# Two tiles of every third group copied on chip instead of every fourth, with ACT joining a column of both tables in one ACTIVATE

## The chip, the cores and the metric

The kernel runs on one core of a Trainium2 chip. The metric is the time on the device in microseconds (us), of which lower is better. The engines are named as the profile names them: PE (TensorE) multiplies matrices, DVE (VectorE), ACT (ScalarE) and POOL (GpSimd) work on elements, and SP issues DMAs. Each has its own queue of instructions and works through it in order.

## The reference

One layer of a graph network with a residual and a layer norm: 12,500 nodes of 64 features, 200,000 edges sorted by destination, 32 features per edge.

```python
msg_in = concatenate([nodes[row], nodes[col], edge_features])   # row = src, col = dst
messages = relu(msg_in @ mW1 + mb1) @ mW2 + mb2
aggregated = segment_sum(messages, col)
out = relu(concatenate([nodes, aggregated]) @ uW1 + ub1) @ uW2 + ub2
x = layernorm(x + out)
```

## The kernel before

The first product is split over its three inputs. Two tables are made at the start: tab_a is x times the source part of mW1, tab_b is x times the destination part. Edges are worked in tiles of 128 and in groups of six tiles; there are 261 groups (index s below), and two groups share what is loaded and selected at once.

*Sources.* For most tiles POOL fetches the rows of tab_a by the edges' source numbers, one indirect DMA per tile (gather, line 207), into the tile xg of the group. The first ten groups fetch rows of x instead. Nine buffers of xg are used in turn, so POOL can run ahead of the work; a buffer is free again after the group's h add.

*Copied tiles.* In the groups of the list COPIED the last two of the six tiles aren't gathered. x lies transposed in SBUF, too: xtop holds it in partitions 0 to 63 with zeros below, xbot in partitions 64 to 127 with zeros above. For a copied group a tile xc of 128 by 128 is put together column by column: the upper half of column e is x of the source of edge e of the fifth tile, the lower half that of edge e of the sixth. PE then multiplies it with w1a (line 366) into the sums of pc. Source numbers are read into registers from two lists that DVE works out once from the column list, `cols` (columns_list, in iteration 9). ACT makes the first 64 columns of xc: for each 32-bit word of its list two COPYs of 64 partitions by one float (lines 328 and 330), for two columns of one half, so 128 COPYs. DVE makes the other 64 columns, each with one bitwise OR of a column of xtop and one of xbot (line 341). The register loads are TENSOR_LOADs (lines 321 and 334; DVE's takes the list in pieces of up to 16 columns, which are 32 words). The work for a copied group is cut into as many shares as there are groups between two copied ones, and `copies(s)` puts one share at the end of each iteration; the last is done two iterations before the group's edge part.

*An iteration s*, with the order written out by hand, puts into the queues: gathers whose buffers are free by then; the norm of an update, if one is due; the destination rows from tab_b (windows); `node_part(s)`, in which DVE adds pc and xg (the h add, line 390, or 386 in a copied group) and ACT applies relu (391, or 387 and 388); `collect(s - 1)`, in which PE sums h into windows of 32 nodes (sums, 418) and counts edges (423); in every second iteration DVE's selections of the next two groups (233, 235, 239) and ACT's cast of one of them (247); `edge_part(s + 1)`, PE's products of destination rows and edge features into pc (363); and the copies.

*Updates.* The sums of up to 448 nodes are kept in PSUM. When a period of nodes ends, ACT takes the sums out (437, 438), PE carries the overlap over (431, 432) and computes the node update (pu, 460 and 461, then py, 469 and 470), DVE takes the statistics (st and mv, 474 and 476), ACT the root (sd, 478), and in the next iteration DVE writes the norm (rs and o, 484 and 487), which frees py's buffer in PSUM for a further pc. As the first nodes have the most edges, periods are long at first (47 groups) and get shorter. New ones begin at groups 47, 66, 81, 93, 104, 114, 123, 131, 139, 146, 153, 160, 166, 172, 178, 184, then every five groups from 190 to 225, and every four to 257.

Of the kernel before, what the change touches and what calls it, by code (L numbers as in the profile page):

```python
# [10 lines left out]
F32 = mybir.dt.float32  # L11
I32 = mybir.dt.int32
AF = mybir.ActivationFunctionType
ALU = mybir.AluOpType
# [3 lines left out]
P = 128  # L18
N, D, DE, DH = 12500, 64, 32, 128
# [10 lines left out]
NSUB = -(-NT // SUB)  # L30
# [39 lines left out]
XBASE = 8320  # L70
U8, U16 = mybir.dt.uint8, mybir.dt.uint16
YBASE = XBASE + 4 * XCOLS
FIRST, GAPS = 20, (4,)
COPIED = []
while FIRST + sum(GAPS) * (len(COPIED) // len(GAPS)) + sum(GAPS[:len(COPIED) % len(GAPS)]) < NSUB - 12:
    COPIED.append(FIRST + sum(GAPS) * (len(COPIED) // len(GAPS)) + sum(GAPS[:len(COPIED) % len(GAPS)]))
RNDS = -(-len(COPIED) // len(GAPS))
SINGLE = 64


def updates():
# [17 lines left out]
def gnn_kernel(ctx: ExitStack, tc: tile.TileContext, x1T, x, eT, e_rows, src, src_row, dst, dst_row, wlist, wrow, wnext, whalf,  # L99
# [24 lines left out]
    nc = tc.nc  # L124
    const = ctx.enter_context(tc.tile_pool(name="const", bufs=1))
# [10 lines left out]
    xbot = const.tile([P, XCOLS], F32, name="xbot")  # L136
# [2 lines left out]
    past = const.tile([1, 1], F32, name="past")  # L139

    cols = const.tile([RNDS * len(GAPS), 2 * P], I32, name="cols")
    col_i = const.tile([RNDS * len(GAPS), SINGLE, 2], U16, name="col_i")
    col_a = const.tile([RNDS * len(GAPS), P - SINGLE, 2], I32, name="col_a")
    w1b = const.tile([P, DH], F32, name="w1b")
    b1 = const.tile([P, DH], F32, name="b1")

# [65 lines left out]
    with tc.tile_pool(name="sup", bufs=2) as sup, tc.tile_pool(name="work", bufs=2) as work, tc.manual_schedule():  # L212
# [73 lines left out]
        def columns_list():  # L286

            for r in range(len(GAPS)):
                v = src_row[:, ((FIRST + sum(GAPS[:r])) * SUB + SUB - 2) * P:]
                nc.sync.dma_start(cols[r * RNDS:(r + 1) * RNDS],  # L290
                                  bass.AP(v.tensor, v.offset, [[sum(GAPS) * SUB * P, RNDS], [1, 2 * P]]))
            cv = cols.rearrange("k (b e) -> k b e", b=2)
            iv = col_i.rearrange("k (b e) h -> k b e h", b=2)
            nc.vector.tensor_scalar(iv[:, :, :, 0], cv[:, :, :SINGLE:2], 4.0, float(XBASE), op0=ALU.mult, op1=ALU.add)
            nc.vector.tensor_copy(iv[:, :, :, 1], cv[:, :, 1:SINGLE:2])
            for b, base in enumerate((XBASE, YBASE)):
                nc.vector.tensor_scalar(col_a[:, :, b], cv[:, b, SINGLE:], 4.0, float(base), op0=ALU.mult, op1=ALU.add)

        x8, y8 = xtop.bitcast(U8), xbot.bitcast(U8)

        def shares(total, n, of):

            at = [-(-total * i // (n * of)) * of for i in range(n + 1)]
            return [(at[i], min(at[i + 1], total)) for i in range(n)]

        def copies(s):

            for j, c in enumerate(COPIED):
                gap = GAPS[(j - 1) % len(GAPS)]
                if c - 2 - gap <= s < c - 2:  # L310
                    break
            else:
                return
            q = s - (c - 2 - gap)
            k = j % len(GAPS) * RNDS + j // len(GAPS)
            if q == 0:
                xc[c] = work.tile([P, P], F32, name="xc")
            o8 = xc[c].bitcast(U8)
            last_a = 4 * (N - 1)
            lo, hi = shares(SINGLE, gap, 4)[q]  # L320
            _, v = nc.values_load_multi_w_load_instructions(  # L321
                col_i.rearrange("k e b -> k (e b)").bitcast(I32)[k:k + 1, lo:hi], engines=[ET.Activation],
                min_val=0, max_val=N * 65536 - 1, skip_runtime_bounds_check_because="sources are node numbers")
            for i, w in zip(range(lo, hi), v):
                b, e = divmod(i, SINGLE // 2)
                o = o8[b * D:b * D + D, 8 * e:8 * e + 8]
                n = (w & 65535).with_bounds(min_val=XBASE, max_val=XBASE + last_a) - XBASE
                nc.scalar.copy(o[:, :4], x8[:D, bass.ds(n, 4)])  # L328
                n = (w >> 16).with_bounds(min_val=0, max_val=N - 1) * 4
                nc.scalar.copy(o[:, 4:], x8[:D, bass.ds(n, 4)])  # L330
            lo, hi = shares(P - SINGLE, gap, 2)[q]
            for a in range(lo, hi, 16):
                m = min(a + 16, hi)
                _, v = nc.values_load_multi_w_load_instructions(
                    col_a.rearrange("k e b -> k (e b)")[k:k + 1, 2 * a:2 * m], engines=[ET.DVE], min_val=XBASE,
                    max_val=YBASE + last_a, skip_runtime_bounds_check_because="sources are node numbers")
                for e in range(a, m):
                    i, n = (w.with_bounds(min_val=base, max_val=base + last_a) - base
                            for w, base in zip(v[2 * (e - a):], (XBASE, YBASE)))
                    w = 4 * (SINGLE + e)  # L340
                    nc.vector.tensor_tensor(o8[:, w:w + 4], x8[:, bass.ds(i, 4)], y8[:, bass.ds(n, 4)],  # L341
                                            op=ALU.bitwise_or)

        xc = {}
# [297 lines left out]
        def rest(s):  # L642
# [5 lines left out]
            if s == 9:  # L648
                columns_list()
# [78 lines left out]
        for s in range(last + 2):  # L728
# [32 lines left out]
            if s + 2 in due:  # L761
                columns(due[s + 2])
            rest(s)
            copies(s)
            if s - 1 in due:
                store(due[s - 1])
# [4 lines left out]
    with tc.If(flag > 0), tc.tile_pool(name="gen", bufs=1) as up:  # L771
# [28 lines left out]
        with tc.For_i(0, NT, 1) as t:  # L800
# [31 lines left out]
            h = up.tile([P, DH], F32, name="hg")  # L832
# [29 lines left out]
        with tc.For_i(0, NB, 1) as c:  # L862
# [24 lines left out]
            o = up.tile([P, D], F32, name="o")  # L887
# [49 lines left out]
```

## Time and profile before

| | |
|---|---|
| runs | 1834.96, 1829.88, 1831.20 us; median 1831.2 |
| profiled execution | 1832.05 us, its span 1830.3 us |
| POOL | busy 1369.6 us (75%), 1447 gathers |
| PE | busy 1440.8 us (79%), mean granted clock 0.577 |
| ACT | busy 1157.8 us (63%), of which copies 1412.8 us summed one by one (they overlap) |
| DVE | busy 856.1 us (47%) |
| DMA | 108 GB/s on average |
| chain that ended last | POOL 36%, issue 23%, PE 19%, DMA 10%, DVE 7%, ACT 3% |

The busy time is the time in which an engine had an instruction under way. Register work, register loads and the issue of DMAs don't count as busy; where an engine stands idle through them, the waits are put down to "issue". In the lines of groups, the numbers behind the bar are the busy time, the mean duration of one instruction in ns, and the idle time just before them with what ended it. The lines of the chain give the start in us, the length in us, and the engine, tile and line.

### The profile page before, as it was taken

The numbers are of one execution on the slowest core, as the hardware profiler recorded it, in microseconds if no ns is written. First come the engines' busy times: TensorE is split into PE (matmuls) and PEld (weight loads), VectorE is DVE, ScalarE is ACT, GpSimd is POOL, SyncE is SP. The second block draws the span as 40 slices with busy tenths as digits, with TensorE's granted clock in tenths as the row PEclk, the third lists the DMA queues.
The fourth block names the chain that finished last, engine by engine and source line by source line (L and its number), as shares of the span: only waits on it lengthen the run. The fifth ranks groups of instructions, "written<-read, shape, count | busy, mean of one in ns | idle before, by whom it ended". The sixth has DMA issues, their size and how long they took to land.

```text
span 1830.3 us, 51040 instructions
## 1 busy us (share of the span) xinstructions
PE 1440.8 (79%) x9446; PEld 1243.3 (68%) x9446; DVE 856.1 (47%) x4895; ACT 1157.8 (63%) x8032; POOL 1369.6 (75%) x1456
## 2 busy tenths in 40 slices
PE   3697897776777777777877788887888888888887
PEld 3586887676666666666766667776766766767765
DVE  1565664454444444435444445444444544544432
ACT  0224886676676767757766667676776776767511
POOL 7777777777777777777777777777777777777774
PEclk8755655555555555555555555555556556566565
DMA  8874444333333333333333333433343433444432
GB/s 212 202 147 123 125 125 120 96 90 91 90 93 94 95 91 94 101 92 98 100 100 102 99 102 100 107 104 100 106 106 101 110 103 101 109 107 108 109 103 63
DMA packets 209512, 197.52 MB, mean 108 GB/s; under 512 B 58284, under 2 KB 174079, under 8 KB 209199
## 3 DMA queue, kind: packets, MB, share of 16 engines
q0 software_dynamic: 46304, 92.96, 20.4%
q1 hardware_dynamic: 148350, 92.34, 18.5%
q10 hardware_dynamic: 14546, 8.93, 1.8%
q8 instruction: 90, 1.47, 0.3%
q14 instruction: 222, 1.82, 0.3%
HBM read 176.40 MB, written 17.66 MB: 106 GB/s over the span
## 4 chain that ended last, share of the span: by engine, by line
POOL 36%; issue 23%; PE 19%; DMA 10%; DVE 7%; ACT 3%; ACTq 1%; DVEq 1%; SPq 1%; POOLq 0%
POOL xg L207 36%; PE sums L418 7%; DMA xg<-tab_a,src_s 5%; PE pc L363 4%; DVE xc L341 2%; PE pu L460 2%; PE pu L461 1%; DMA tab_a<-tb 1%; DMA l<-in_dst_row 1%; DVE h L390 1%; DVE l L235 1%; PE py L469 1%; PE py L470 1%; ACTq L321 1%; ACT xc L328 1%
## 5 line engine op out<-in xcount | busy, mean ns | idle before, releaser
L207 POOL DMA_INDIRECT xg<-tab_a,src_s x1387 | 1310.8, 945 | 422.7 <-issue 402.0
L418 PE MATMUL sums<-sel,h 128*128 128x32 f32 x3126 | 665.9, 381 | 191.7 <-ACT h L391 186.7
L418 PEld LDWEIGHTS sums<-sel,h 128*128 128x128 f32 x3126 | 635.5, 307 | 254.5 <-ACT h L391 228.8
L328 ACT COPY xc<-xtop 64x4 uint8 x3712 | 698.4, 188 | 114.1 <-issue 112.8
L330 ACT COPY xc<-xtop 64x4 uint8 x3712 | 714.4, 192 | 10.9 <-issue 10.9
L363 PE MATMUL pc<-rhs,l 64*128 64x128 f32 x3126 | 421.5, 424 | 134.8 <-DVE o L487 113.4
L363 PEld LDWEIGHTS pc<-rhs,l 64*128 64x128 f32 x3126 | 349.9, 305 | 191.7 <-DVE o L487 117.1
L341 DVE TENSOR_TENSOR xc<-xtop,xbot 128x4 uint8 x3712 | 299.6, 155 | 278.4 <-issue 278.1
L390 DVE TENSOR_TENSOR h<-pc,xg 128x768 f32<-128x768 f32 (+1 forms) x194 | 183.6, 947 | 355.5 <-DMA xg<-tab_a,src_s 263.4
L391 ACT ACTIVATE h<-h 128x768 f32<-128x768 f32 (+1 forms) x194 | 162.2, 837 | 245.9 <-DVE h L390 235.4
L235 DVE TENSOR_TENSOR l<-l,cps 128x768 f32<-128x768 int32 (+1 forms) x134 | 127.8, 954 | 29.4 <-DMA l<-in_dst_row 25.1
L247 ACT CAST selb<-sel 128x384 bf16<-128x384 f32 x131 | 66.1, 505 | 68.0 <-DVE sel L239 62.0
L474 DVE BATCH_NORM_STATS2 st<-py 128x6 f32<-128x64 f32 x131 | 20.5, 218 | 145.0 <-PE py L470 141.7
L423 PE MATMUL cnt<-selb,one 128*1 128x32 bf16 x1563 | 84.8, 188 | 0.0
L239 DVE TENSOR_TENSOR sel<-cps,drc 128x384 f32<-128x384 f32 x131 | 71.9, 549 | 20.2 <-PE sums L418 19.3
L478 ACT ACTIVATE sd<-mv,eps 128x4 f32<-128x4 f32 (+1 forms) x33 | 9.8, 297 | 109.4 <-DVE mv L476 109.4
L207 POOL DMA_INDIRECT xg<-in_x,src_s x60 | 57.7, 962 | 19.1 <-issue 18.0
L423 PEld LDWEIGHTS <-one 128*1 128x1 bf16 x1563 | 54.0, 83 | 22.5 <-issue 8.7
L386 DVE TENSOR_TENSOR h<-pc,xg 128x512 f32<-128x512 f32 x58 | 39.8, 686 | 49.4 <-DMA xg<-tab_a,src_s 29.5
L460 PE MATMUL pu<-sums_s,w2u 128*128 128x448 f32 (+1 forms) x66 | 61.2, 1032 | 0.5 <-ACT sums_s L437 0.5
L469 PE MATMUL py<-ux,xw 128*128 128x64 f32 x262 | 54.0, 289 | 5.1 <-ACT hTu L462 4.9
L470 PE MATMUL py<-u,hTu 128*128 128x64 f32 x262 | 52.5, 283 | 0.4 <-ACT hTu L462 0.4
(105 smaller groups left out, 857.3 us busy)
## 6 DMA issues: line engine op xcount, KB each, us to landing
l<-in_dst_row SPq DMA_DIRECT2D x262, 96.0 KB
l<-in_eT SPq DMA_DIRECT2D x262, 96.0 KB
xg<-tab_a,src_s POOLq DMA_INDIRECT x1387
rhs<-tab_b SPq DMA_DIRECT2D x361, 32.0 KB
tab_b<-tb SPq DMA_DIRECT2D x13, 512.0 KB
rhs<-tab_b SPq DMA_DIRECT2D x387, 16.0 KB
tab_a<-tb ACTq DMA_DIRECT2D x12, 512.0 KB
out<-o SPq DMA_DIRECT2D x32, 128.0 KB
```

The costliest lines, as they stand in the source:

```text
L207: nc.gpsimd.indirect_dma_start(out=a[:, i, :] if s < XG else a[:, i // 2, i % 2, :], out_offset=None, in_=A[:, :] if s >= XG else x[:, :], ...
L235: nc.vector.tensor_tensor(l[r], l[r].bitcast(I32), node[r].unsqueeze(2).broadcast_to([r.stop - r.start, SUP // 2, P]), op=ALU.is_equal)
L328: nc.scalar.copy(o[:, :4], x8[:D, bass.ds(n, 4)])
L330: nc.scalar.copy(o[:, 4:], x8[:D, bass.ds(n, 4)])
L341: nc.vector.tensor_tensor(o8[:, w:w + 4], x8[:, bass.ds(i, 4)], y8[:, bass.ds(n, 4)], op=ALU.bitwise_or)
L363: nc.tensor.matmul(pc[:, b, k, :], L[g][q:q + 64, m, :], rhs[g % 2][q:q + 64, w, :], start=s >= XG or k == 0, stop=s >= XG and not copied)
L390: nc.vector.tensor_tensor(h[:, b, :m], pc[:, b, :m], a[:, b, :m], op=ALU.add)
L391: nc.scalar.activation(h[:, b, :m], h[:, b, :m], AF.Relu)
L418: nc.tensor.matmul(ps[:, bass.ds(ws[i], WIN)], h[:, i % 2, i // 2, :], S[g][:, k0 + i, :], start=False, stop=ends and i == n - 1)
L423: nc.tensor.matmul(pn[:, bass.ds(ws[i], WIN)], one, SB[g][:, k0 + i, :], start=False, stop=ends and i == n - 1)
L460: nc.tensor.matmul(pu, w2u, sums_s[u % 2][:, :n], start=True, stop=False)
L469: nc.tensor.matmul(py[:, i], xw[u % 2][:, i * P:(i + 1) * P], ux, start=True, stop=False)
```

## The change

Copied groups go from every fourth, from the 20th to the 248th (58 groups), to every third, from the 16th to the 253rd (80 groups). ACT's part of a column list becomes 60 columns and DVE's 68, in three shares instead of four. ACT's columns are made by one ACTIVATE each: its input is the column of xtop and its bias the column of xbot, so that both halves are written at once. The list for ACT changes its form with that: each 32-bit word holds the place in xtop in its lower half and the node number for xbot in the upper half.

```diff
-FIRST, GAPS = 20, (4,)
+FIRST, GAPS = 16, (3,)
...
-while FIRST + ... < NSUB - 12:
+while FIRST + ... < NSUB - 6:
...
-SINGLE = 64
+ACTS = 60
...
-            iv = col_i.rearrange("k (b e) h -> k b e h", b=2)
-            nc.vector.tensor_scalar(iv[:, :, :, 0], cv[:, :, :SINGLE:2], 4.0, float(XBASE), op0=ALU.mult, op1=ALU.add)
-            nc.vector.tensor_copy(iv[:, :, :, 1], cv[:, :, 1:SINGLE:2])
+            nc.vector.tensor_scalar(col_i[:, :, 0], cv[:, 0, :ACTS], 4.0, float(XBASE), op0=ALU.mult, op1=ALU.add)
+            nc.vector.tensor_copy(col_i[:, :, 1], cv[:, 1, :ACTS])
...
-            lo, hi = shares(SINGLE, gap, 4)[q]
+            lo, hi = shares(ACTS, gap, 4)[q]
...
-            for i, w in zip(range(lo, hi), v):
-                b, e = divmod(i, SINGLE // 2)
-                o = o8[b * D:b * D + D, 8 * e:8 * e + 8]
-                n = (w & 65535).with_bounds(min_val=XBASE, max_val=XBASE + last_a) - XBASE
-                nc.scalar.copy(o[:, :4], x8[:D, bass.ds(n, 4)])
-                n = (w >> 16).with_bounds(min_val=0, max_val=N - 1) * 4
-                nc.scalar.copy(o[:, 4:], x8[:D, bass.ds(n, 4)])
-            lo, hi = shares(P - SINGLE, gap, 2)[q]
+            for e, w in zip(range(lo, hi), v):
+                i = (w & 65535).with_bounds(min_val=XBASE, max_val=XBASE + last_a, guaranteed_mod_val=0, out_of_modulus=4) - XBASE
+                n = (w >> 16).with_bounds(min_val=0, max_val=N - 1)
+                nc.scalar.activation(xc[c][:, e:e + 1], x8[:, bass.ds(i, 4)].bitcast(F32), AF.Identity,
+                                     bias=xbot[:, bass.ds(n, 1)])
+            lo, hi = shares(P - ACTS, gap, 2)[q]
             for a in range(lo, hi, 16):
                 m = min(a + 16, hi)
```

In the rest of the function SINGLE becomes ACTS.

More of the change, by code (lines that the diff above doesn't have):

```diff
@@ L72 @@
 YBASE = XBASE + 4 * XCOLS
-FIRST, GAPS = 20, (4,)
+FIRST, GAPS = 16, (3,)
 COPIED = []
-while FIRST + sum(GAPS) * (len(COPIED) // len(GAPS)) + sum(GAPS[:len(COPIED) % len(GAPS)]) < NSUB - 12:
+while FIRST + sum(GAPS) * (len(COPIED) // len(GAPS)) + sum(GAPS[:len(COPIED) % len(GAPS)]) < NSUB - 6:
     COPIED.append(FIRST + sum(GAPS) * (len(COPIED) // len(GAPS)) + sum(GAPS[:len(COPIED) % len(GAPS)]))
 RNDS = -(-len(COPIED) // len(GAPS))
-SINGLE = 64
+ACTS = 60
 def updates():
@@ L141, in gnn_kernel @@
     cols = const.tile([RNDS * len(GAPS), 2 * P], I32, name="cols")
-    col_i = const.tile([RNDS * len(GAPS), SINGLE, 2], U16, name="col_i")
-    col_a = const.tile([RNDS * len(GAPS), P - SINGLE, 2], I32, name="col_a")
+    col_i = const.tile([RNDS * len(GAPS), ACTS, 2], U16, name="col_i")
+    col_a = const.tile([RNDS * len(GAPS), P - ACTS, 2], I32, name="col_a")
     w1b = const.tile([P, DH], F32, name="w1b")
@@ L292, in columns_list @@
             cv = cols.rearrange("k (b e) -> k b e", b=2)
-            iv = col_i.rearrange("k (b e) h -> k b e h", b=2)
-            nc.vector.tensor_scalar(iv[:, :, :, 0], cv[:, :, :SINGLE:2], 4.0, float(XBASE), op0=ALU.mult, op1=ALU.add)
-            nc.vector.tensor_copy(iv[:, :, :, 1], cv[:, :, 1:SINGLE:2])
+            nc.vector.tensor_scalar(col_i[:, :, 0], cv[:, 0, :ACTS], 4.0, float(XBASE), op0=ALU.mult, op1=ALU.add)
+            nc.vector.tensor_copy(col_i[:, :, 1], cv[:, 1, :ACTS])
             for b, base in enumerate((XBASE, YBASE)):
-                nc.vector.tensor_scalar(col_a[:, :, b], cv[:, b, SINGLE:], 4.0, float(base), op0=ALU.mult, op1=ALU.add)
+                nc.vector.tensor_scalar(col_a[:, :, b], cv[:, b, ACTS:], 4.0, float(base), op0=ALU.mult, op1=ALU.add)
         x8, y8 = xtop.bitcast(U8), xbot.bitcast(U8)
@@ L339, in copies @@
                             for w, base in zip(v[2 * (e - a):], (XBASE, YBASE)))
-                    w = 4 * (SINGLE + e)
+                    w = 4 * (ACTS + e)
                     nc.vector.tensor_tensor(o8[:, w:w + 4], x8[:, bass.ds(i, 4)], y8[:, bass.ds(n, 4)],
```

## The prediction

> **What bounds the kernel now.** I read the groups by shape first, then the waits, then single source lines, and last the chain of waits in a late stretch. The groups:
>
> ```profile
> L207 POOL DMA_INDIRECT xg<-tab_a,src_s x1387 | 1310.8, 945 | 422.7 <-issue 402.0 <-DMA xg<-tab_a,src_s 10.4 <-DVE xc L341 3.0
> L330 ACT COPY xc<-xtop 64x4 uint8 x3712 | 714.4, 192 | 10.9 <-issue 10.9
> L341 DVE TENSOR_TENSOR xc<-xtop,xbot 128x4 uint8 x3712 | 299.6, 155 | 278.4 <-issue 278.1
> L478 ACT ACTIVATE sd<-mv,eps 128x4 f32<-128x4 f32 x32 | 9.5, 297 | 106.1 <-DVE mv L476 106.1
> ```
>
> POOL never waits: 945 ns busy and 0.30 us of issue per gather, so one starts every 1.2495 us in the timeline. All 1447 gathers (60 read x) take 1808 of the 1830.3 us. Before such a gather its buffer has been free for some 50 us from group 48 on, nine groups being buffered. So POOL sets the time, as long as the consumers (DVE's h add, ACT's relu, PE's sums) hold its pace of 22 gathers, 27.49 us, per four groups. Do they? The chain from 1560 to 1720 us:
>
> ```profile
> 1612.36 2.02 issue
> 1614.38 1.26 DVE xc L341 x16
> 1616.92 1.81 PE pc L363 x12
> 1619.15 2.70 PE sums L418 x12
> 1622.10 1.58 PE pc L363 x12
> 1623.69 2.70 PE sums L418 x12
> 1626.64 1.58 PE pc L363 x12
> 1628.76 2.77 PE sums L418 x12
> 1632.94 1.79 PE pu L460 x2
> 1634.73 1.20 PE pu L461 x2
> 1635.93 0.87 PE pc L363 x12
> 1638.76 0.62 DVE st L474 x4
> 1639.67 2.02 issue
> 1641.69 1.28 DVE xc L341 x16
> ```
>
> No gather is in it. Here an update comes every four groups, and from one xc to the next pass 27.31, 27.57 and 27.98 us: 27.6, POOL's own pace. The consumers are full too. The loop runs: PE's py, DVE's st, the list load and copies that stand before the norm, norm, h add, relu, copies, relu, copies, relu, sums, update, py. PE and ACT both run through without a gap in its middle. So there are two limits at nearly the same height, and the change lowers one and raises the other.
>
> **The change part by part.** *Gathers.* Copied groups: 58 (20 to 248) become 80 (16 to 253), so 44 gathers go: 44 x 1.2495 = 55.0 us off POOL, none of it covered. POOL alone would give 1832.05 - 55.0 = 1777 us. (The profiled execution took 1832.05, 0.85 over the median of the runs shown.) Its new pace is 16 gathers per three groups, 6.66 us per group against 6.87.
>
> *Lists and copies: the lines.*
>
> ```profile
> L334 DVEq TENSOR_LOAD <-col_a x232: 2097/2152/2719, 159.8 to 1709.2; - x116
> L321 ACTq TENSOR_LOAD <-col_i x232: 1010/1034/1424, 158.2 to 1710.8; - x116
> L328 ACTq ALU_OP  x3712: 35/35/49, 159.5 to 1715.1; - x196
> L330 ACTq FUSED_REGOPS  x3712: 64/67/83, 159.6 to 1715.2; - x196
> ```
>
> *DVE, per group.* Today 16 columns: one load of 32 words (2.15 us), of which the waits show 278.1/232 = 1.2 us, then 16 copies 73 ns apart. After it 68 columns over three steps, cut in pairs: 24, 22, 22; the inner loop takes 16 at a time, so a second load follows. A load of one word takes 0.312 us (line 769), 32 take 2.15, so 59 ns a word and 0.96 to 1.20 us for 12 or 16 words. In today's trace a load starts with four or five copies still queued, which hides 0.3; seen: 0.65 to 0.9. With six or eight more copies (0.44, 0.58) a step grows by 1.05 to 1.45, I take 1.2. Bounds: 0.5, if the load were hidden as the first half of today's is, and 2.6, if it cost a whole 2.15.
>
> *ACT, per group.* Today 16 words give 32 copies in 3.46 us (single rows of the timeline, 105 ns apart, 188 to 192 ns long). Each word costs the sequencer 35 and 67 ns of register work and two dispatches, 209 ns by the trace's starts. After it 20 words give 20 ACTIVATEs of 128x1 with a register for the input and one for the bias. No such instruction is in the trace, so its spacing is bounded. From below: 155 ns, if the two register operations follow each other without a gap and one dispatch (53 ns) remains. From above by the sequencer: 209, if dropping a dispatch saves nothing. By the engine: sd is the nearest row, 297 ns for four elements with a bias against 192 for four without, so a bias adds 105; copies overlap by 92, which leaves 205 if the bias is not overlapped, and about 100 if it is. I take 190 ns, between 155 and the two upper ends but nearer these, as sd is the only row of the same form. That makes 20 x 0.19 + 0.1 = 3.9 us, and four more words in the load 0.2 (50 ns a word, by 286 ns for one and 1034 for 16). An ACT step grows by 0.64 us (bounds: -0.06 at 155 ns, 1.02 at 209).
>
> The Trainium skill (ScalarE: Activation LUTs, What ACT_TABLE_LOAD costs) speaks against the new form: a pointer bias adds about 93 ns to an ACTIVATE, and neighbours overlap by about 93, so one with a bias takes the room of two without. By its figures the spacing would be an estimated 187 ns, the step 0.06 us less than mine and the sum some 3 us lower; sd's 105 ns agrees with the rule.
>
> *PE.* Each copied group adds four matmuls of 64x128, 0.80 us in the timeline, now in every third group: 0.07 us per group. In the late loop PE will wait for ACT, which covers it; uncovered it is 0.27 per four groups. *Start.* Copies begin at iteration 11 instead of 14, while the consumers still trail by 30 to 39 us. The buffer of a gather there is free 18 to 27 us early; three steps and a slower catch-up take some 15 of that. I count nothing, at worst 5 us. The column list (80 rows for 58) goes by the same single DMA on SP, and its conversions stay four DVE operations of about 0.19 us.
>
> *The sum.* The late loop holds one DVE step (py waits for the norm, and edge_part, sums and the next h add are queued behind both) and two ACT steps (relu is queued behind the copies, and PE's sums wait for relu): 27.6 + 1.2 + 2 x 0.64 = 30.1 us per four-group period, where POOL now needs 26.66. A further group in a longer period costs an ACT step: 4.66 to 4.95 us between relus today, 5.4 after, against POOL's 6.66. So the consumers fall back by 3.4 us in a four-group period, 2.2 in one of five (35.5 against 33.3), 0.9 in one of six (40.9 against 40.0), and hold in one of seven. By the list of updates there are five of six groups (160 to 190), seven of five (to 225) and 6.5 of four until copying ends at iteration 250: 4.5 + 15.4 + 22.1 = 42 us. That fits into the 50 us of buffers, so POOL does not stop, but the lag is added at the end. From group 252 on POOL needs 49 x 1.2495 = 61.2 us, and the consumers, without load and copies in their loop (27.6 - 3.3 = 24.3 per four groups, 6.1 each), 54.9: 6.3 are won back. Net 55.0 - 42 + 6.3 = 19.3 us: 1832.05 - 19.3 = 1812.7, **1813 us**.
>
> **The rivals.** *The consumers keep up.* If ACTIVATEs start 155 ns apart, an ACT step does not grow, and PE's own chain binds: 27.6 + 1.2 + 0.27 = 29.1 per four groups and 4.9 for a further one. The lag is 6.5 x 2.4 + 7 x 0.7 = 20, less 6: 1791; with the DVE load hidden as well 1785, and 1777 is the floor. For it: the step drops twelve of 32 instructions. Against it: each column keeps both register operations, and sd's 297 ns.
>
> *The ACT step grows past the gain: slower.* The place is the copies between two relus. The turning point: at 205 ns a step grows by 0.94, the periods fall back by 4.0, 3.1, 2.1 and 1.2 us (four to seven groups), together 62, and the gain is gone: 1832. A further register operation of 35 ns for the bias's address, or for reading bytes as floats, would make it 225 ns: 31.5 per four groups, 6.1 for each further one, so that all periods of up to eleven groups fall back, together 99: 1832 - 55 + 99 - 6 = 1870 us. Were the bias read wholly serial at 297 ns, every group would be ACT's, and it would be over 1950. For it: 205 and 209 are my own upper ends, 15 ns from my value. Against it: today's shift and multiply already share one operation of 67 ns, and the new address needs the same two.
>
> *The change doesn't do what it says* would need POOL to stop gaining, by stalls at the start; that is priced above at 5 us and no case of its own.
>
> **How the numbers follow.** Forecast, 1790 to 1835: 0.50. Consumers keep up, 1777 to 1790: 0.17. ACT past the gain, above 1835: 0.33. The predicted time is the first one's, 1813. Its own range of 1790 to 1835 covers the bounds of the two steps nearest to it. The range given, 1782 to 1880, reaches into both rivals: the lower leaves out 0.07, the upper 0.12 (over 225 ns). A difference of 0.3%, 5.5 us, is about what a measurement of this kernel can tell from none, so faster ends at 1825.7 and slower begins at 1836.7. Of the forecast's 0.50, 0.41 is faster, 0.07 same, 0.02 slower; the second gives 0.17 faster; of the third 0.03 is same, 0.30 slower. Together 0.58, 0.10, 0.32.
>
> **What would show it.** In the profile of the changed kernel: 1343 gathers from tab_a, still 945 ns, but now with idle time that names DVE if the lag passes 50 us; h add's waits for gathers (263.4 us today) falling most after 1100 us; the ACTIVATEs some 190 ns apart, 20 in 3.9 us; two list loads per step, the second near 1.0 us; the chain of waits through ACT's xc from about group 160. A spacing above 205 ns, or POOL waiting for DVE's h adds over much of the second half, makes me wrong on the slow side; gathers that set h add's start to the end, on the fast side.

## The result: 0.3% slower

The changed kernel takes 1836.49 us (median of 7 runs, 1834.92 to 1838.37), the kernel before 1830.36 in the same comparison (1829.39 to 1834.96). The ratio is 1.003, with a 95% interval of 1.0018 to 1.0041: a small loss where a gain of 1% was forecast. The profiled execution took 1838.37 us, its span 1836.6, 6.3 more than the span of before. (The ratios here and below leave out one slow execution, of e4_one_load, that took 1891.81 us where its other three took 1823.74 to 1827.31.)

Groups by shape, after:

```profile
L207 POOL DMA_INDIRECT xg<-tab_a,src_s x1343 | 1273.3, 948 | 421.2 <-issue 386.1 <-DMA xg<-tab_a,src_s 11.9 <-DVE h L387 10.1
L326 ACT ACTIVATE xc<-xtop,xbot 128x1 f32 x4800 | 973.6, 290 | 172.5 <-issue 166.0 <-DMA u<-in_uW 6.5
L338 DVE TENSOR_TENSOR xc<-xtop,xbot 128x4 uint8 x5440 | 450.8, 156 | 407.0 <-issue 406.0
L387 DVE TENSOR_TENSOR h<-pc,xg 128x768 f32<-128x768 f32 x170 | 162.4, 955 | 74.2 <-DMA xg<-tab_a,src_s 24.6 <-PE pc L360 23.3 <-issue 8.7
```

The 44 gathers are gone, and the rest cost nearly what they did, 948 ns on average instead of 945. Two entries have changed: POOL now waits for DVE's h adds (10.1 us, against 1.5 before), and the h adds wait 24.6 us for gathers where the waits of the kernel before have:

```profile
DVE h L390 <- DMA xg<-tab_a,src_s: 263.4, 87, 7.0
```

The gathers no longer lead.

Single source lines (duration in ns: least, median, most; then the start of the first and of the last). First line: the kernel before; the others: after.

```profile
L207 POOL DMA_INDIRECT xg<-tab_a,src_s x1387: 940/944/1973, 78.9 to 1811.1; - x199
```
```profile
L207 POOL DMA_INDIRECT xg<-tab_a,src_s x1343: 942/947/1870, 78.9 to 1772.1; - x192
L320 ACTq TENSOR_LOAD <-col_i x240: 1236/1275/1701, 130.0 to 1763.2; - x120
L326 ACTq ALU_OP  x4800: 35/35/49, 131.8 to 1768.6; - x192
L331 DVEq TENSOR_LOAD <-col_a x480: 843/2052/2533, 124.8 to 1765.7; - x160
```

The last starts of the gathers give the account. POOL's saving of 55.0 us would bring the last gather from 1811.1 to 1756.1; it starts at 1772.1, so it is 16.0 us *late*. From the last gather to the end of the span it was 1830.3 - 1811.1 = 19.2 us and is now 1836.6 - 1772.1 = 64.5, so the *tail* is 45.3 longer. 16.0 + 45.3 - 55.0 = 6.3, the whole difference. These two numbers are given below for every kernel. Not all of the 16.0 us is waiting. In three places, shown below, POOL waits for an h add, 11.1 us beyond its pace; the other 5 us or so are the gathers themselves, which start 1.252 us apart (median) where before's start 1.249 apart. In e1 and e4 below the gathers are as slow, POOL never waits so, and the last gather is 4.5 and 4.7 us late all the same.

When the time was lost is seen from the start of the h adds against the kernel before: 30.0 us earlier at group 160, 23.4 at 190, 9.3 at 226, then 8.7 *later* at group 250. The lag of an h add behind the last gather of its group, taken just before an update, is 14.2 us at group 48 (1.7 before), as the work there still trails from the start, stays at 2 to 3.4 us from group 67 to 161, and is then 5.8, 8.1, 10.8, 13.2 and 15.8 (at 191), 36.5 at 226 and 54.7 at 250. Towards the end of this the buffers are used up, as POOL's timeline shows (start, length, idle time before it and what ended it; a third such wait, of 3.35 us, ends at 1738.97):

```profile
1677.45 0.95 POOL L207 DMA_INDIRECT xg<-tab_a,src_s  x1 [5.05 <-DVE h L387]
1708.34 0.95 POOL L207 DMA_INDIRECT xg<-tab_a,src_s  x1 [3.64 <-DVE h L387]
```

The chain of waits of after, in the same stretch as shown for before:

```profile
1608.84 0.62 DVE st L471 x4
...
1609.74 1.98 issue
1611.72 0.67 DVE xc L338 x8
1612.46 0.56 DVE xc L338 x7
1613.02 0.45 issue
1613.47 0.70 DVE xc L338 x8
...
1615.39 0.88 DVE h L387
1616.35 0.84 ACT h L388
1617.20 0.76 ACTq L320
...
1622.14 0.61 ACT h L384
...
1628.80 2.77 PE sums L415 x12
...
1639.94 0.63 DVE st L471 x4
```

From one st to the next pass 31.1 us, where POOL needs 26.66 for four groups. Between st and the h add stand two list loads (1.98 and 0.45 us of issue) and 24 copies. The relus of three groups follow at 1616.35, 1622.14 and 1627.92, 5.8 us apart, with ACT's list load and its 20 ACTIVATEs between them. In before's chain PE's pc and sums filled this middle; here PE waits for ACT.

### The profile page after: what moved, and what is told of

The parts are those of the page before. It is cut to its first block, busy times and chain, and to the rows that moved or that the text cites. A ratio compares the mean times of both kernels' runs of the same rounds, so it can differ in the third digit from the quotient of the medians.

```text
span 1836.6 us, 52710 instructions
## 1 busy us (share of the span) xinstructions
PE 1437.5 (78%) x9534; PEld 1236.9 (67%) x9534; DVE 1001.0 (55%) x6623; ACT 1305.7 (71%) x5430; POOL 1331.9 (73%) x1412
## 4 chain that ended last, share of the span: by engine, by line
POOL 23%; issue 22%; PE 18%; ACTq 8%; DVE 8%; DMA 6%; ACT 6%; DVEq 2%; SPq 0%; POOLq 0%
POOL xg L207 23%; PE sums L415 6%; DMA xg<-tab_a,src_s 5%; ACTq L326 5%; ACT xc L326 4%; ACTq L320 3%; PE pc L360 3%; DVE xc L338 3%; PE pu L457 2%; PE pu L458 2%; DVEq L331 1%; PE py L466 1%; DVE h L387 1%; PE py L467 1%; DVE l L235 1%
## 5 line engine op out<-in xcount | busy, mean ns | idle before, releaser
L207 POOL DMA_INDIRECT xg<-tab_a,src_s x1343 | 1273.3, 948 | 421.2 <-issue 386.1
L326 ACT ACTIVATE xc<-xtop,xbot 128x1 f32 x4800 | 973.6, 290 | 172.5 <-issue 166.0
L415 PEld LDWEIGHTS sums<-sel,h 128*128 128x128 f32 x3126 | 626.3, 303 | 249.2 <-ACT h L388 157.7
L338 DVE TENSOR_TENSOR xc<-xtop,xbot 128x4 uint8 x5440 | 450.8, 156 | 407.0 <-issue 406.0
L387 DVE TENSOR_TENSOR h<-pc,xg 128x768 f32<-128x768 f32 (+1 forms) x172 | 163.0, 948 | 74.2 <-DMA xg<-tab_a,src_s 24.6
L388 ACT ACTIVATE h<-h 128x768 f32<-128x768 f32 (+1 forms) x172 | 142.0, 827 | 58.3 <-DVE h L387 58.3
L247 ACT CAST selb<-sel 128x384 bf16<-128x384 f32 x131 | 65.8, 502 | 40.2 <-DVE sel L239 37.3
L207 POOL DMA_INDIRECT xg<-in_x,src_s x60 | 57.6, 960 | 19.2 <-issue 17.7
L457 PE MATMUL pu<-sums_s,w2u 128*128 128x448 f32 (+1 forms) x66 | 61.2, 1032 | 0.5 <-ACT sums_s L434 0.5
L383 DVE TENSOR_TENSOR h<-pc,xg 128x512 f32<-128x512 f32 x80 | 55.1, 689 | 10.6 <-DMA xg<-tab_a,src_s 7.8
L363 PE MATMUL pc<-w1a,xc 64*128 64x128 f32 x320 | 60.3, 397 | 0.0
L459 ACT ACTIVATE hTu<-pu,ub_s 128x448 f32<-128x448 f32 (+1 forms) x33 | 20.9, 633 | 49.8 <-PE pu L458 49.8
L458 PE MATMUL pu<-xw,uz 128*128 128x448 f32 (+1 forms) x66 | 54.1, 924 | 0.0
```

The source lines that it names most:

```text
L207: nc.gpsimd.indirect_dma_start(out=a[:, i, :] if s < XG else a[:, i // 2, i % 2, :], out_offset=None, in_=A[:, :] if s >= XG else x[:, :], ...
L326: nc.scalar.activation(xc[c][:, e:e + 1], x8[:, bass.ds(i, 4)].bitcast(F32), AF.Identity, bias=xbot[:, bass.ds(n, 1)])
L387: nc.vector.tensor_tensor(h[:, b, :m], pc[:, b, :m], a[:, b, :m], op=ALU.add)
L388: nc.scalar.activation(h[:, b, :m], h[:, b, :m], AF.Relu)
L415: nc.tensor.matmul(ps[:, bass.ds(ws[i], WIN)], h[:, i % 2, i // 2, :], S[g][:, k0 + i, :], start=False, stop=ends and i == n - 1)
L457: nc.tensor.matmul(pu, w2u, sums_s[u % 2][:, :n], start=True, stop=False)
```

## The experiments

The theory: the consumers' loop, with two ACT steps and one DVE step in each update period, has become slower than POOL from group 160 on; the lag fills the buffers, and at the end it has to be worked off. The rivals: the new ACTIVATEs cost by themselves wherever they are; or the longer list does, by what it does at the start, on PE or in the DMAs.

All ratios are to the kernel before, in runs of the same comparison:

| kernel | gathers saved | ratio, 95% interval | last gather late, us | tail, us |
|---|---|---|---|---|
| before | 0 | 1 | 0 | 19.2 |
| after | 44 | 1.003 [1.0018, 1.0041] | 16.0 | 64.5 |
| e1_form_alone | 0 | 0.9999 [0.9989, 1.0008] | 4.5 | 17.7 |
| e2_list_alone | 44 | 1.0147 [1.013, 1.0164] | 41.9 | 64.0 |
| e3_no_bias | 44 | 0.9803 [0.9787, 0.9819] | 0.5 | 36.5 |
| e4_one_load | 44 | 0.9948 [0.9928, 0.9967] | 4.7 | 64.7 |
| e5e_dve_first | 44 | 0.9822 [0.9806, 0.9839] | -0.7 | 38.9 |
| e7c_late_fourth | 22 | 0.9858 [0.984, 0.9876] | 0.0 | 19.2 |
| e8d_both | 32 | 0.9782 [0.9766, 0.9799] | 0.1 | 18.9 |

The last two columns are from the profiled executions, worked out as above (1811.1 less 1.25 us per gather saved is the start that a last gather would have). The gathers of after, e1, e2 and e4 take 948 ns on average and start 1.252 to 1.253 us apart, those of the others 944 to 946 ns and 1.249 us, so in these four rows some 5 us of the first column are slower gathers and no wait. Why there are two paces is open.

### The two halves of the change, one by one

e1, in after: ACT's new form with the old list (58 groups) and ACT's old share of 64 columns.

```diff
-FIRST, GAPS = 16, (3,)        -ACTS = 60      (... < NSUB - 6)
+FIRST, GAPS = 20, (4,)        +ACTS = 64      (... < NSUB - 12)
```

> The new ACT form with the old list (58 groups, every fourth, 64 columns for ACT, so 16 ACTIVATEs a step). Two limits: POOL sets the time, the consumers (h add, relu, sums, update) follow at its pace. The ACT step is 16 x 0.19 = 3.1 us of copies against 3.46, DVE and the gathers are as before: 1828 to 1831 us, no change. The form itself costs: if ACTIVATEs with a bias register slowed ACT or its neighbours by more than the 0.3 us gained, the late periods would lag and it would be over 1836.

e2, in before: the new list (80 groups) with the old form, ACT making 60 columns by pairs of COPYs.

```diff
-FIRST, GAPS = 20, (4,)        -SINGLE = 64    (... < NSUB - 12)
+FIRST, GAPS = 16, (3,)        +SINGLE = 60    (... < NSUB - 6)
```

> The new list (80 groups, every third, 60 columns for ACT) with the old form, two COPYs per word. The list makes the loss: ACT's step has 40 COPYs at 209 ns a pair, 4.2 us, against 4.0 to 4.3 for 20 ACTIVATEs measured in the changed kernel, so the same late lag, 1836 to 1850 us. The form makes the loss: with COPYs instead the kernel falls clearly below 1830.

Measured: e1 0.9999, e2 1.0147. In e1 a share of 16 columns took 3.32 us on average against 3.57 before, and its h adds still waited 263.7 us for gathers: the gathers set the time, and a shorter share beside them is worth nothing. In e2 a share took 4.43 us, and the consumers held POOL back most, in ten places by 37 us in all (groups by shape, e2):

```profile
L207 POOL DMA_INDIRECT xg<-tab_a,src_s x1343 | 1273.0, 948 | 447.5 <-issue 383.1 <-DVE h L390 22.8 <-DVE cps L233 11.0
```

So, by the ratios, the list alone is a loss of 27 us, more than was expected (1862.83 us against 1836 to 1850), and the new form takes 21 of them back. The form does not cost by itself; it is worth nothing until the list makes ACT's share part of the bound.

### Less in ACT's step, less in DVE's step

e3 leaves out the lower half of ACT's 60 columns, so its ACTIVATEs read no bias, and of the two register operations of each only the ALU_OP of 35 ns is left.

```diff
-                nc.scalar.activation(..., AF.Identity, bias=xbot[:, bass.ds(n, 1)])
+                nc.scalar.activation(..., AF.Identity)
```

> The changed kernel without the bias of ACT's ACTIVATE and its register work; this leaves out the lower half of ACT's 60 columns of each copied pair. ACT's step falls from 4.0-4.3 to about 2.1 us of ACTIVATEs (one register operation and one dispatch, 88 to 100 ns each). If ACT's step between two relus is what binds the late periods, they shrink from 30.7 us per four groups to the 29 of PE and DVE, and the time falls to 1785-1800 us. If DVE's step binds, ACT's relief is hidden and it stays above 1820.

e4 makes one list load on DVE instead of two per share: columns after the 16th read the sources of the first ones again, and so leave out their own.

```diff
+                if a == lo:
                   _, v = nc.values_load_multi_w_load_instructions(
```

> The changed kernel with one list load per DVE share: the six or eight columns after the sixteenth use the first ones' registers again, which leaves out their own sources. A DVE step is 0.65 to 0.9 us shorter. ACT's step binds between relus and DVE's only before the norm: once per period, so some 20 late periods x 0.8 = 16 us, 1820 us. DVE binds every step: two to three times that, below 1800. No part of DVE's step counts: 1836.

Measured: e3 0.9803, e4 0.9948. The groups by shape of e3:

```profile
L326 ACT ACTIVATE xc<-xtop 128x1 f32 x4800 | 485.2, 189 | 205.9 <-issue 196.9 <-DVE sel L239 9.1
```

Without the bias one ACTIVATE takes 189 ns instead of 290 and the next follows after 94 instead of 197; a share falls from 4.14 to 2.07 us. The four-group period, from one update's st to the next, falls from 30.6 to 28.4 us on average, and POOL is no longer held back. That is 42 us for 2.07 us per share. It does not reach POOL's floor of 1777: a lag of 22 us is left at group 250, and in its late chain PE's sums and pc are the longest lines, 27.7% and 22.1% of the stretch from 1560 to 1720 us.

In e4 the same number of copies with one load less shortened the periods by 0.5 to 0.6 us, and the time by 15 us (0.8% between the two ratios), as expected for a load that counts once per late period. Either step, made shorter, brings the time down: both are in the chain, as the theory has it.

### DVE's share out of the norm's way

Nothing is left out here, nor in the kernels that follow. In the iterations in which an update is due, DVE's share goes into its queue ahead of the update's st instead of between st and the norm, the rest as in after.

```diff
+            if s in due:
+                copies(s, act=False)
             residual(due[s])
...
-            copies(s)
+            copies(s, dve=s not in due)
```

> The changed kernel with one thing moved: where an update is due, DVE's share of the copies is queued ahead of the update's statistics (where DVE waits for PE's py, 218.9 us in all) instead of between them and the norm. If the loop ACT copies, relu, sums binds the late periods, the norm comes 4.7 us earlier but relu then waits for ACT's own copies, which end some 6.6 us after the statistics begin, against 7.6 to 8 today: 1.0 to 1.4 us per late period, 20 to 30 us in all, ratio to the kernel before 0.987 to 0.992. If the wait for the norm itself binds, all 4.7 us per period come off and POOL is the limit again, 0.975. If neither, 1.003.

Run again as e5b, e5c and e5d:

> The changed kernel with DVE's share ahead of the update's statistics, again, because in the first run the kernel before took 2832 us, with single register operations of up to 1.6 us on ACT. Expected as there: 0.987 to 0.992 if ACT's own copies bind relu once the norm comes earlier, 0.975 if the wait for the norm alone binds, 1.003 if neither.

> The changed kernel with DVE's share ahead of the update's statistics, in the state of the result (the kernel before near 1830 us). 0.987 to 0.992 of the kernel before if ACT's own copies bind relu once the norm comes earlier, 0.975 if the wait for the norm alone binds, 1.003 if neither.

> The changed kernel with DVE's share ahead of the update's statistics, in the state of the result (the kernel before near 1830 us). Its periods would fall from 30.7, 36.4 and 42.5 us (four, five and six groups) by 1.0 to 1.4 each if ACT's own copies bind relu once the norm comes earlier: 0.987 to 0.992 of the kernel before. By 4.7 if the wait for the norm alone binds: 0.975. Unchanged, 1.003, if neither.

And as e5e:

> The same kernel as before, on a chip where the kernel before takes about 1830 us. The theory that a DVE share standing between st and h is paid once in each update (1.1 to 1.2 us against the kernel before's 5.35) gives 170/3.. no more than about 30 periods of some 0.6 to 1.2 us: 0.985 to 0.995 of the kernel before. The rival, that the share only moves its wait to another place, gives 1.000 to 1.005.

The first four runs of this kernel, and seven of its kin (the same move made in the kernel before, and the first runs of the two kernels below), were made on four other chips, on which the kernel before itself took 2830 to 2922 us, and the longest register operation on ACT 1.4 to 1.7 us, by run. The gathers don't set the time there: in e5 POOL waited 421.5 us for DVE's h adds, where it waits 10.1 in after. So their ratios (0.9937, 0.9825, 0.9993 and 0.9928 for this one) tell of another bound and are used for nothing here.

Measured with the kernel before at 1831.05 us: 0.9822. The h add after the st of 1608.84 in after, then DVE's timeline of e5e:

```profile
1615.31 0.95 DVE L387 TENSOR_TENSOR h<-pc,xg 128x768 f32<-128x768 f32 x1
```
```profile
1573.18 0.62 DVE L472 BATCH_NORM_STATS2 st<-py 128x6 f32<-128x64 f32 x4 [3.53 <-PE py L468]
1573.73 0.36 DVE L474 BATCH_NORM_AGGREGATE mv<-st 128x2 f32<-128x6 f32 x4
1574.45 0.18 DVE L482 RECIPROCAL rs<-sd 128x4 f32<-128x4 f32 x1 [0.36 <-ACT sd L476]
1574.67 1.10 DVE L485 TENSOR_SCALAR o<-py,mv,rs 128x64 f32<-128x64 f32 x4
1575.68 0.95 DVE L388 TENSOR_TENSOR h<-pc,xg 128x768 f32<-128x768 f32 x1
```

From st to the h add pass 2.50 us instead of the 6.47 of after's timeline (1608.84 to 1615.31). The whole DVE step is out of the chain, not only what the change added to it, and the gain (38 us against after) is larger than the expectation had it (0.985 to 0.995). A period shrank less than the 4.0 us: by 1.3 us with four groups, 2.3 with five, 2.4 with six. Those of six groups are now at POOL's own pace (40.2 us for the 40.0 that their gathers need). In the shorter ones ACT weighs more: its list loads, register work and ACTIVATEs are 29% of the chain from 1560 to 1720 us by its lines, where they are 23% in after. The lag at group 250 is 21.6 us instead of 54.7. The rival, that the share only moves its wait elsewhere, is out.

The same move in the kernel before was run only on two of those other chips, where it gave 0.9773 and 0.9715; what it does where the gathers set the time was not measured.

> The kernel before with the same move. If POOL alone sets its time, nothing changes (0.998 to 1.001), though the waits for the norm shrink. If the late update periods set it, as the chain from 1560 to 1720 us could also be read, it gains 10 us or more.

> The kernel before with the same move, again: 0.998 to 1.001 if POOL alone sets its time, 0.994 or less if its late update periods do.

### A list that is thinner where the updates are dense

e7, e7b and e7c are the same kernel: every third group from 16 to 136, every fourth from 140 to 248, with ACT making 64 columns (24, 20 and 20 in three shares, 16 each in four). DVE's share is in its old place.

```diff
-FIRST, GAPS = 16, (3,)
+SEGS = ((16, 137, 3), (140, 249, 4))
+COPIED = [c for a, b, g in SEGS for c in range(a, b, g)]
```

> The changed kernel with every third group copied only up to group 136 and every fourth from 140 to 248 (69 groups; 64 columns for ACT). If the loss arises only in the short update periods after group 139, the 22 gathers saved until there stay saved: 22 x 1.2495 = 27.5 us, ratio 0.985. If the longer list costs time everywhere (the start, the loads), 0.995 or more.

> Every third group copied up to group 136, every fourth from 140, again: 0.985 if the loss arises only in the short update periods, 0.995 or more if the longer list costs time everywhere.

> Two tiles copied in every 3rd group from 16 to 136 and in every 4th from 140 to 248 (69 groups, 22 gathers fewer than the kernel before), with ACT's new form, DVE's share in its old place. If the lag of the loop behind the gathers is what the changed kernel loses, and it grows only where updates come every six groups or fewer with every 3rd group copied, no lag is left at the end here and all 22 gathers are won: 1832.05 - 22 x 1.2495 = 1804.6 us in the profiled execution, 0.984 to 0.988. If the ACT form or the longer DVE share cost by themselves, whatever the updates' spacing, more than half of the 27 us is lost: 0.993 or above.

Measured: 0.9858, median 1804.44 us, the profiled execution 1804.59 where 22 gathers less make 1804.6. The gathers of e7c:

```profile
L204 POOL DMA_INDIRECT xg<-tab_a,src_s x1365: 938/944/998, 79.8 to 1783.6; - x195
```

The last gather starts 27.5 us earlier than before, all of the saving, and the tail is before's 19.2 us to the tenth. Its lag is 25.9 us at group 48 and still 12.7 at group 132, where after has 14.2 and 1.9 (a share of 24 columns takes ACT 4.96 us, one of 20 takes 4.14); by group 147 it is 3.1, and it does not come back. So neither the form nor the start of copying at group 16 costs anything that lasts: the loss lies in the late part of the list. (The first two runs of this kernel, on the other chips told of above, gave 1.0107 and 1.0007.)

e8, e8b, e8c and e8d have DVE's share moved as in e5 and the list every third to 190, then every fourth to 250 (74 groups), with ACT making 64 columns.

```diff
+SEGS = ((16, 191, 3), (194, 251, 4))
```

> Both edits together, with every third group up to 190 and every fourth from 194 to 250 (74 groups, 64 columns for ACT). 32 gathers fewer than before are 40 us; the periods of six groups lose about 1.2 us each after the move, the late ones win that back: ratio 0.978 to 0.982. If the six-group periods still fall back as in the changed kernel, 0.985 or more.

> Both edits, every third group up to 190, again: 0.978 to 0.982 if the move takes 1.0 to 1.4 us off each period; 0.985 or more if the six-group periods still fall back as in the changed kernel.

> The move, and every third group only up to 190, in the state of the result: 0.978 to 0.982 if the move takes 1.0 to 1.4 us off each period; 0.985 or more if the six-group periods still fall back as in the changed kernel.

> The same kernel as before, on a chip where the kernel before takes about 1830 us. If the lag theory holds, the four-group spacing at the end stops the lag from growing past group 194 and the time is 0.980 to 0.995 of the kernel before; if the lag is not what costs, 1.000 or above.

Measured: 0.9782, median 1791.33 us, the best of all (its first three runs, on the other chips, gave 1.0096, 0.9925 and 1.0049). Its 32 saved gathers are 40.0 us, and 1832.05 - 40.0 = 1792.1 is what the profiled execution took (1791.95). The lag rises to 16.1 us at group 185, where every third group is still copied, and is about 2 from group 216 on. In e5e, with the same list up to there but 60 columns for ACT, it is 2.4 at group 185: the shares of 24 columns make that lag. The thinner late list with 60 columns was not run. The chain of waits of e8d from 1560 to 1720 us, by line, begins with the gathers again:

```profile
by line: POOL xg L204 58.2%; issue 34.6%; DMA xg<-tab_a,src_s 2.1%; DVE xc L338 1.9%; DVEq L331 1.3%; DVE l L232 1.2%; DVE sel L236 0.3%; DVE cps L230 0.3%; DVE h L387 0.2%; DVEq L387 0.1%
```

## Why the prediction was wrong, step by step

**POOL.** 44 gathers at 1.25 us, right: where the consumers kept up (e7c, e8d) the saved gathers came off within 2 us. "POOL does not stop" was wrong: it waited 11.1 us, as the lag outgrew the buffers.

**The start.** Nothing was lost, as taken: the h add of group 160 starts 30.0 us earlier than before. The 26 gathers saved up to there are 32.5 us, and the 2.5 that are missing are an estimated 0.003 us for each of some 810 gathers, the slower pace told of above.

**DVE's step.** Taken at +1.2 us; from group 139 on, st to h add is 6.5 us with a share of 24 columns and 6.1 with one of 22, against 5.3 in before, so +0.8 to +1.2, on average +1.0. The second list load takes some 0.86 or 1.12 us (12 or 16 words) where 0.96 to 1.20 was estimated.

**ACT's step is the term that failed.** The mechanism was right, and this term of its sum was too small: it was taken at +0.64 us and is +0.92. Of that, a share takes 4.14 us on average instead of 3.57 (4.04 and 3.46 at the median), so +0.57, where 3.9 against 3.46, +0.44, had been taken: the ACTIVATEs start 197 ns apart, not 190. The list load is 1.275 against 1.034, +0.24 (+0.2 taken). From the load to the first copy pass 0.25 instead of 0.145 us at the median, +0.11, which was not in the sum. The bound of 209 ns from the sequencer was the right place to look: 35 + 67 ns of register operations leave 95 ns for the gaps and the dispatch. Only where ACT's queue was filled ahead do 20 ACTIVATEs take less:

```profile
1629.54 3.82 ACT L326 ACTIVATE xc<-xtop,xbot 128x1 f32 x20
```

That is (3.82 - 0.29) / 19 = 186 ns, where the Trainium skill (ScalarE: Activation LUTs, What ACT_TABLE_LOAD costs) gave an estimated 187: its rule for the engine holds here, and the bias adds 101 ns (290 against e3's 189). But the sequencer set the usual 197, as in this row its ALU_OPs still start 196 to 197 ns apart, and with the rule's value the sum would have been further off. The 94 ns of e3 can't tell the two apart, as a register operation of 67 ns left with the bias.

**The sum.** The missing 0.28 us count two, three and four times in a period of four, five and six groups. Periods of four, five and six groups became 30.6, 36.5 and 42.6 us on average where 30.1, 35.5 and 40.9 were forecast; a further group cost 5.9 to 6.1 us, not 5.4, as relus are up to 5.8 us apart and 7.4 where ACT's cast waits for DVE's selection ahead of the list load. At group 250 the 42 saved gathers before it are 52.5 us, and its h add came 8.7 us later than before, so the consumers lost 61.2 us there and not 42: 19.2 of the miss. With the prediction's counts of periods, 0.28 us per ACT step makes an estimated 15 us of it (6.5 x 0.56 + 7 x 0.84 + 5 x 1.12), and 2.5 were lost to the slower gathers before group 160. 6.3 us were to be won back after the copying; at group 260 the loss is 55.0 + 3.6 = 58.6, so 2.6 were, and then the end came 6.3 us later, not 3.6. These give 19.2 + 3.7 + 2.7 = 25.6 us, and the span is 6.3 over instead of 19.3 under.

**The rivals.** The second named the mechanism, the place and the point: a step of +0.94 eats the gain, 62 us of it, and gives 1832 us. The step came out at 0.92, the loss at 61.2 us and the time at 1838 in the profiled execution; that they agree so closely is in part luck, as 2.5 of the 61.2 us are the slower gathers. What had been tied to it, a spacing of 205 ns, was not reached; the step got there by the load and the gap ahead of the first copy. The first rival, 155 ns, is refuted by the measured 197.

**What was not asked.** The DVE step was priced by what the change adds (1.0 us), not by what it is (6.1 to 6.5 us in a chain that has just become the bound). Moving it was worth more than the whole miss.

## What to carry to other kernels

When an engine that feeds buffers runs at the pace of the loop that empties them, a saving on the one is paid only as far as the other has slack, so compute the slack of each stage of the run and spend the change where it is: with 22 gathers saved instead of 44, all before group 139, the kernel became 1.4% faster instead of 0.3% slower. Price a step of register-addressed instructions as load, gap to the first, and count times the spacing of the sequencer, from means of many rows; a quarter of a us, two to four times per period, is an estimated 15 us here, and the sign with it. And look at what stands in the new bound's chain for another reason, for moving one share of copies in its queue was worth 2.1%.

## What the hardware showed that was not expected

- Register-addressed ACTIVATEs with a bias start 197 ns apart (median) and 186 when queued ahead; without the bias and its register operation 94. The sequencer's two register operations for each take 35 and 67 ns.
- The same gather had two paces: 948 ns and one per 1.252 us in after, e1, e2 and e4, 945 ns and one per 1.249 us in the other profiles above. What sets them is open.
- On four chips the kernel before took 2830 to 2922 us instead of 1830: ACT's register operations, 35 and 67 ns at the median, went up to 1.7 us, and POOL waited 460.7 us for DVE's h adds (in the kernel before with the share moved). What causes it is open.
